# Last image's z loaded row by row of the kernel window, 32 channels outermost; its output parts in the tiles of y

## The chip, the cores and the metric

The kernel runs on one core of one Trainium2 chip. The metric is the device time of one execution in microseconds (us); the time of a kernel is the median of several runs. One profiled execution gives the trace; its span, from the first instruction to the last, is a little shorter than the time of that execution.

## What is computed

Two layers work on 16 images of 56 x 56 pixels with 384 channels. The first normalises the image in 32 groups of channels, makes q, k and v with a 1x1 convolution, lets every pixel attend to 9 neighbours (at distance 1, 2 or 3, a third of the channels each), projects the result and adds it to the image. The second normalises again, convolves each channel by itself with a 3x3 kernel of values -1, 0, 1, and adds.

```
x = x + _L0_conv_ref(_gn(x), L0_conv_w_qkv, L0_conv_w_proj, L0_conv_b_proj)
x = x + _L1_conv_ref(_gn(x), L1_conv_w)      # depthwise 3x3, 'SAME', binary kernel
```

## The kernel before

An image is cut into 7 chunks of 8 rows (PX = 448 pixels); 16 images give 112 chunks. Channels lie on the 128 partitions in 3 groups (j = 0, 1, 2). Each chunk passes three plans: plan A loads x, turns it to channels first, takes statistics and writes it to a buffer in device memory (xd); plan B is the attention and writes its result to x1d; plan C is the second layer and writes the output. Plan C of an image can only normalise when the statistics of the whole image after plan B are known.

The pieces of all plans are put on a grid of slices, sorted by slice and kind, and recorded in that order; a scheduler then orders them within each engine, and each engine works through its own list in order. So plans A and B of later images lie beside plan C of earlier ones. Only the last image (b = B - 1) has its plan C alone: nothing is left to run beside it. It fills the last 140 us of the span, and this stretch is called the tail here.

What plan C does with one chunk, with the lines:

- L745 (`load_g`) loads xg_last, the third group of channels, with a row above and below. L719 (`load_x`) loads x, the first two groups, 128 partitions of 2 x 448 values.
- `load(j)` for j = 0, 1 loads z: for each of 4 sets q of 32 channels, the same 32 channels three times, on partitions 0-31, 32-63 and 64-95, each a row of the image further (ky = 0, 1, 2). So a matmul over 96 partitions sums the three kernel rows. In the last image z has two tiles for each j, with two sets each (`z_last`); the tiles are those of t in even chunks and of w (one of xr) in odd ones, free by then. The first and the last chunk of the image are loaded by L694, one DMA for each ky and tile: 32 channels x 2 sets x 448. The chunks between are loaded by L702, one DMA for each set q, whose source pattern is written by hand with the three rows ky outermost: 3 x 32 x 448.
- L713 on ACT normalises three of the four sets of each j, L709 on DVE the fourth (q = 3); L715 on POOL clears edges in the first and the last chunk. L756 on ACT normalises xg_last into zg.
- L727 (`convolve`) is 12 matmuls for each j (24 records in the trace) into the PSUM tile pc, the q = 3 one first; L734 on DVE adds pc to x.
- L769 on DVE is the nine taps of the third group, each adding to the one before (m, at last xg_last).
- L799 (`turn`) transposes four parts of 112 pixels into pt_o, L801 on ACT copies each into osb, and in the last image L804 issues the output DMA from ACT's queue. osb is a tile of pool o_p, which has 2 buffers. pc and pt_o share three PSUM buffers.

The scheduler gives the completion of each DMA one of eight semaphores in turn, over the queues of SP and ACT together. A DMA waits until the one that had its semaphore before has landed. The built program's list shows these waits.

In the tail, PE's list is: convolve chunk c (j = 0, 1), turn chunk c - 1 (four parts), convolve chunk c + 1, and so on; at the end come the turns of chunks 5 and 6.

Of the kernel before, what the change touches and what calls it, by code (L numbers as in the profile page):

```python
# [8 lines left out]
F32 = mybir.dt.float32  # L9
# [8 lines left out]
P = 128  # L18
# [4 lines left out]
NQ = 4  # L23
ROWS = 8
SUB = 112
# [10 lines left out]
def dilated_attention_then_binary_conv(  # L36
# [28 lines left out]
    nc = tc.nc  # L65
    B, H, W, C = x.shape
    PX = ROWS * W
    NCH = H // ROWS
# [82 lines left out]
    y_p = ctx.enter_context(tc.tile_pool(name="y_p", bufs=4))  # L151
# [5 lines left out]
    o_p = ctx.enter_context(tc.tile_pool(name="o_p", bufs=2))  # L157
# [497 lines left out]
    def plan_c(m, t0):  # L655

        b, c = divmod(m, NCH)
        p0 = c * PX
        had = {}

        def edges(j):
            found = []
            for z, _, _ in had[f"z{j}"]:
                if c == 0:
                    found.append(z[0:HD, :, 0:W])
                if c == NCH - 1:
                    found.append(z[2 * HD : 3 * HD, :, PX - W : PX])
            return found

        def set_of(j, q):  # L670
            return next(z[:, q - q0] for z, q0, q1 in had[f"z{j}"] if q0 <= q < q1)

        def load(j):
            by_set = x1d[b].rearrange("(j q c) n -> j c q n", q=NQ, c=HD)[j]
            if b < B - 1:
                z = z_p.tile([P, NQ * PX], F32, tag="z", name="z")[:K3].rearrange("p (q n) -> p q n", q=NQ)
                had[f"z{j}"] = [(z, 0, NQ)]
            else:

                had[f"z{j}"] = []  # L680
                for q0 in range(0, NQ, 2):
                    pool, tag = (t_p, "t") if c % 2 == 0 else (w_p, "w") if (j, q0) != (1, 2) else (xr_p, "xr")
                    z = pool.tile([P, 3, PX], F32, tag=tag, name="z_last")[:K3, :2]
                    had[f"z{j}"].append((z, q0, q0 + 2))
            for edge in edges(j):
                nc.gpsimd.memset(edge, 0.0)
            for ky in range(3):
                lo = W if c == 0 and ky == 0 else 0
                hi = PX - W if c == NCH - 1 and ky == 2 else PX
                n0 = p0 + (ky - 1) * W  # L690
                for z, q0, q1 in had[f"z{j}"]:
                    if b == B - 1 and 0 < c < NCH - 1:
                        continue
                    nc.sync.dma_start(  # L694
                        z[ky * HD : (ky + 1) * HD, :, lo:hi], by_set[:, q0:q1, n0 + lo : n0 + hi]
                    )
            if b == B - 1 and 0 < c < NCH - 1:

                for q in range(NQ):
                    one = by_set[:, q, p0 - W : p0 - W + PX]  # L700
                    three_rows = bass.AP(one.tensor, one.offset, [(W, 3), *one.ap])
                    nc.sync.dma_start(set_of(j, q), three_rows)  # L702

        def normalise(j):
            mrz = mr1[b][1]
# [88 lines left out]
        def turn(s):  # L794
            pt = ps_mt.tile([P, 512], F32, tag="mt", name="pt_o")
            mid = had["xg"][:, 1 : ROWS + 1, :].rearrange("p r w -> p (r w)")
            for j in range(NG):
                src = mid if j == JG else had["x1"][:, j]
                nc.tensor.transpose(pt[:SUB, j * P : (j + 1) * P], src[:, s * SUB : (s + 1) * SUB], ident)  # L799
            osb = o_p.tile([SUB, C], F32, tag="osb", name="osb")  # L800
            nc.scalar.copy(osb, pt[:SUB, :C])  # L801

            queue = nc.sync if b < B - 1 else nc.scalar
            queue.dma_start(of[b, p0 + s * SUB : p0 + (s + 1) * SUB, :], osb)  # L804

        if b == B - 1:

            at(t0 - 12, LOADS, load_g)
            at(t0 - 3, LOADS, load_x)
            ahead = 8 if c else 1  # L810
            at(t0 - ahead, NORM, normalise_g)
            for j in range(JG):
                at(t0 - 12 + j, LOADS, lambda j=j: load(j))
                at(t0 - ahead + j, NORM, lambda j=j: normalise(j))
                at(t0 + 1 + j, CONVOLVE, lambda j=j: convolve(j))
            for ky in range(3):
                at(t0 + 1 + ky, CONVOLVE, lambda ky=ky: taps_last(ky))
            for s in range(NSUB):
                at(t0 + 12, STAGE_C, lambda s=s: turn(s))
            return  # L820
# [9 lines left out]
        for j in range(JG):  # L830
            at(t0 - 4 + 3 * j, LOADS, lambda j=j: load(j))
            at(t0 - 1 + 3 * j + late, NORM, lambda j=j: normalise(j))
            at(t0 + 2 + 3 * j + late, CONVOLVE, lambda j=j: convolve(j))
        for s in range(NSUB):
            at(t0 + 9 + s, STAGE_C, lambda s=s: turn(s))
# [51 lines left out]
```

## Time and profile before

| | us |
|---|---|
| median of 3 runs (lowest, highest) | 5411.35 (5409.35, 5414.15) |
| the profiled execution, its own time | 5406.89 |
| its span | 5405.2 |
| PE busy in the span | 5205.9 (96%) |
| DVE, POOL, ACT busy | 4150.0, 4215.2, 2397.8 |
| mean granted TensorE clock | 0.98 of full speed |
| normalising of the last image starts | at 5269.5 |
| convolve of chunk 1 ends (PE) | at 5293.7 |
| convolve of chunk 2, 3, 4, 5 starts | at 5300.55, 5323.03, 5345.41, 5369.80 |
| convolve of chunk 6 ends | at 5391.8 |
| last output copy starts (ACT) | at 5401.41 |

How to read the views used below. "SPq" and "ACTq" are the queues in which SP and ACT issue DMAs; the time of such a row is that of issuing, not of the transfer. In the chain of waits, each piece is what the next one waited for, followed back from the last instruction; the trace gives a landing as the time between issue and what it released. In a timeline, a row gives the start, the time until the last of its instructions ended, engine, line, operation, out<-in, and the count. PEclk is the granted share of the TensorE clock, "DMA share" the mean busy share of the 16 DMA engines.

### The profile page before, as it was taken

Reading aid. Unit: us, or ns where it says so; the run is one execution under the profiler, and the core shown is the slowest. Engines: PE = TensorE matmul, PEld = TensorE weight load, DVE = VectorE, ACT = ScalarE, POOL = GpSimd, SP = SyncE. Lnnn points to the kernel's source line nnn. Section 1 sums busy time; section 2 is a strip of 40 time slices with the busy share of each in tenths; the row PEclk is TensorE's granted clock in tenths of the full one; section 3 lists DMA queues with packets and bytes.
Section 4 is the critical chain, followed back from the end, with each engine's and each line's share of the span. In section 5 each row is a group of like instructions: output and inputs, shape, how many; then the busy total and the mean of one; then the engine's idle time right before and its main releaser. Section 6 shows DMA issues by size and latency. Waiting matters only on the chain. (4 is left out here: it accounts for less than half of the span.)

```text
span 5405.2 us, 77297 instructions
## 1 busy us (share of the span) xinstructions
PE 5205.9 (96%) x27669; PEld 2414.4 (45%) x27669; DVE 4150.0 (77%) x4209; ACT 2397.8 (44%) x4189; POOL 4215.2 (78%) x3049
## 2 busy tenths in 40 slices
PE   8999999999999999999999999999999999999965
PEld 4444444444444444444444444444444444444422
DVE  4887777878777787777777777787777778777754
ACT  3224444444444444444444444444444444444433
POOL 2677888888888887888888788888888888888880
PEclk9999999999999999999999999999999999999976
DMA  5444555655555555555655655555555655544443
GB/s 168 127 120 124 159 157 158 163 154 161 158 158 160 164 159 159 157 157 158 163 154 161 164 152 160 164 157 163 159 157 154 164 154 161 161 130 134 122 130 126
DMA packets 810799, 825.73 MB, mean 153 GB/s; under 512 B 359467, under 2 KB 800174, under 8 KB 810414
## 3 DMA queue, kind: packets, MB, share of 16 engines
q1 hardware_dynamic: 802430, 808.79, 54.2%
q10 hardware_dynamic: 7984, 12.00, 0.7%
q8 instruction: 219, 3.59, 0.3%
q14 instruction: 166, 1.36, 0.1%
HBM read 466.41 MB, written 231.21 MB: 129 GB/s over the span
## 5 line engine op out<-in xcount | busy, mean ns | idle before, releaser
L597 POOL TENSOR_TENSOR w<-w 128x1344 f32<-128x1344 f32 x672 | 2049.9, 3050 | 456.2 <-DVE w L589 396.7
L589 DVE TENSOR_TENSOR w<-pb_a,v 128x1344 f32<-128x1344 f32 x1008 | 1559.1, 1547 | 267.0 <-PE pb_a L582 177.4
L516 DVE TENSOR_TENSOR t<-pq,k 128x1344 f32<-128x1344 f32 x1008 | 1535.8, 1549 | 237.0 <-PE pq L463 236.1
L463 PE MATMUL pkv<-xn,wqkvT 128*128 128x448 f32 x3924 | 1569.9, 549 | 9.0 <-ACT xa L424 4.7
L463 PEld LDWEIGHTS pkv<-xn,wqkvT 128*128 128x128 f32 x3924 | 718.4, 190 | 671.8 <-issue 629.4
L615 PE MATMUL po<-y,wprojT 128*128 128x448 f32 x2016 | 834.9, 550 | 27.4 <-POOL y L601 15.0
L784 POOL TENSOR_TENSOR m<-m 128x1344 f32<-128x1344 f32 x210 | 644.7, 3070 | 274.1 <-ACT m L778 274.0
L463 PE MATMUL pq<-xn,wqkvT 128*128 128x448 f32 x1962 | 830.7, 558 | 0.0
L713 ACT ACTIVATE z<-z,mrz 96x448 f32<-96x448 f32 x840 | 578.3, 751 | 350.9 <-DMA z<-x1d 330.3
L501 PE MATMUL ps<-t,sel 128*32 128x448 f32 x6048 | 666.0, 550 | 26.0 <-DVE t L516 25.3
L778 ACT ACTIVATE m<-zg,ktap 128x448 f32<-128x448 f32 x945 | 555.5, 658 | 274.0 <-POOL m L784 266.9
L615 PEld LDWEIGHTS po<-y,wprojT 128*128 128x128 f32 x2016 | 376.4, 191 | 382.9 <-issue 341.1
L727 PE MATMUL pc<-z,kdiag 96*32 96x440 f32 (+1 forms) x5040 | 516.7, 543 | 6.4 <-POOL z L715 4.6
L463 PEld LDWEIGHTS pq<-xn,wqkvT 128*128 128x128 f32 x1962 | 344.0, 189 | 316.9 <-issue 316.9
L734 DVE TENSOR_TENSOR x<-pc,x 128x448 f32<-128x448 f32 x224 | 139.3, 622 | 353.2 <-PE pc L727 342.1
L582 PE MATMUL pb_a<-aT,spread 24*128 24x448 bf16 x3024 | 369.1, 359 | 32.2 <-DVE w L589 25.9
L601 POOL TENSOR_TENSOR y<-y,w 128x448 f32<-128x448 f32 x336 | 381.5, 1135 | 22.6
L618 DVE SCALAR_TENSOR_TENSOR xr<-po,bias,xr 128x448 f32<-128x448 f32 x336 | 227.5, 677 | 220.9 <-PE po L615 217.2
L600 POOL TENSOR_TENSOR y<-w 128x448 f32<-128x448 f32 x336 | 382.2, 1138 | 14.7
L473 ACT COPY v<-pkv 128x448 f32<-128x448 f32 x336 | 178.3, 531 | 484.1 <-PE pkv L463 475.8
L473 ACT COPY k<-pkv 128x448 f32<-128x448 f32 x336 | 178.2, 530 | 376.5 <-PE pkv L463 376.5
L501 PEld LDWEIGHTS ps<-t,sel 128*32 128x32 f32 x6048 | 170.6, 110 | 364.9 <-issue 247.8
(131 smaller groups left out, 4394.7 us busy)
## 6 DMA issues: line engine op xcount, KB each, us to landing
z<-x1d SPq DMA_DIRECT2D x570, 224.0 KB
xr<-xd SPq DMA_DIRECT2D x112, 672.0 KB
x1d<-xr SPq DMA_DIRECT2D x112, 672.0 KB
xn<-xd SPq DMA_DIRECT2D x109, 672.0 KB
xin<-in_x_dram SPq DMA_DIRECT2D x108, 672.0 KB
xd<-xa SPq DMA_DIRECT2D x315, 224.0 KB
out_dram<-osb SPq DMA_DIRECT2D x420, 168.0 KB
x<-x1d SPq DMA_DIRECT2D x112, 448.0 KB
```

The costliest lines, as they stand in the source:

```text
L463: nc.tensor.matmul(dst[:, :PX], wqkvT[:, cc, o0 : o0 + P], had["xn"][:, cc, :], start=(cc == 0), stop=(cc == NG - 1))
L501: return nc.tensor.matmul(had["ps"][32 * j : 32 * j + 32, :PX], sel[:, s0 : s0 + 32], tk, start=(issued[j] == 1), stop=(issued[j] == len(r ...
L516: nc.vector.tensor_tensor(t.rearrange("p k (r w) -> p k r w", w=W), q3, k3, ALU.mult)
L589: nc.vector.tensor_tensor(w.rearrange("p k (r w) -> p k r w", w=W), pb[:, :, :PX].rearrange("p k (r w) -> p k r w", w=W), three(kv[1][g][m ...
L597: nc.gpsimd.tensor_tensor(w0, w0, w, ALU.add)
L600: nc.gpsimd.tensor_tensor(y, w0[:, 0], w0[:, 1], ALU.add)
L601: nc.gpsimd.tensor_tensor(y, y, w0[:, 2], ALU.add)
L615: nc.tensor.matmul(po[:, :PX], wprojT[:, g, j * P : (j + 1) * P], had[f"y{g}"], start=(g == 0), stop=(g == NG - 1))
L713: nc.scalar.activation(z, z, AF.Identity, bias=mrz[:, j, q, 0:1], scale=mrz[:, j, q, 1:2])
L727: return nc.tensor.matmul(pcr[q * HD : (q + 1) * HD, :, lo:hi], kdiag[:, kx, j * NQ + q, :], rows(set_of(j, q))[:, :, lo + kx - 1 : hi + k ...
L778: nc.scalar.activation(rows(t[:, kx]), zp[:, ky : ky + ROWS, kx : kx + W], AF.Copy, scale=ktap[:, o : o + 1])
L784: nc.gpsimd.tensor_tensor(had["m"], had["m"], t, ALU.add)
```

## The change

In `load(j)`, the middle chunks of the last image lose their own way: the branch with the hand-written pattern (L702) and the `continue` that led to it are gone, so that all chunks go through L694. For chunks 1 to 5 that is 3 (ky) x 2 (tiles) = 6 DMAs of 32 x 2 x 448 for each j in place of 4 of 3 x 32 x 448, with the same bytes. In `turn`, the last image's osb is a view of a tile of pool y_p, which has 4 buffers and whose own use, in plan B, is over by then; other images keep o_p.

```diff
                 for z, q0, q1 in had[f"z{j}"]:
-                    if b == B - 1 and 0 < c < NCH - 1:
-                        continue
                     nc.sync.dma_start(
                         z[ky * HD : (ky + 1) * HD, :, lo:hi], by_set[:, q0:q1, n0 + lo : n0 + hi]
                     )
-            if b == B - 1 and 0 < c < NCH - 1:
-
-                for q in range(NQ):
-                    one = by_set[:, q, p0 - W : p0 - W + PX]
-                    three_rows = bass.AP(one.tensor, one.offset, [(W, 3), *one.ap])
-                    nc.sync.dma_start(set_of(j, q), three_rows)
...
-            osb = o_p.tile([SUB, C], F32, tag="osb", name="osb")
+            if b < B - 1:
+                osb = o_p.tile([SUB, C], F32, tag="osb", name="osb")
+            else:
+                osb = y_p.tile([P, PX], F32, tag="y", name="osb_last")[:SUB, :C]
             nc.scalar.copy(osb, pt[:SUB, :C])
```

In the built programs the lists of PE and POOL are the same but for two rows of POOL (clearing of edges) that change places, and the lists of DVE, ACT and SP are the same up to the start of the tail. In the tail the scheduler orders them anew. Before, the normalising of a chunk and the copies of the turn before it are mixed on ACT and on DVE. After, from chunk 2 on, ACT's list is: two copies, two output DMAs, two copies, two output DMAs (turn of chunk c - 2), six times L713 (chunk c), L756 (chunk c + 1). DVE's list is: L709 twice (chunk c), L734 (c, j = 0), three taps of chunk c + 1, L734 (c, j = 1), six taps of chunk c + 1, L709 twice (chunk c + 1). On SP's queue, a chunk is x (c), xg_last (c + 1), 12 loads of z (c + 1); the output DMAs on ACT's queue take their turn among the eight semaphores between the loads of z.

## The prediction

> **What bounds the kernel now.** Over the whole span PE is busy 96%, but only the tail is changed. I read the chain of waits from 5293 to 5345 first, because it tells what ends last there (start, time, what):
>
> ```profile
> by line: DMA z_last<-x1d 95.3%; SPq L702 4.0%; issue 1.6%; ACT osb L801 0.9%; PE pt_o L799 0.9%; ACT z_last L713 0.0%; ACTq L801 0.0%
> ...
> 5293.74 12.89 DMA z_last<-x1d
> ...
> 5306.64 25.25 DMA z_last<-x1d x2
> ...
> 5331.96 11.44 DMA z_last<-x1d
> ```
>
> Landings of z are 95% of it: the tail is bound by transfers, not by an engine. Next, busy time by engine in two whole chunks of that stretch (engines, then PEclk, DMA share, GB/s):
>
> ```profile
> 5300.50:5345.40 44.90, 23.35 (x120) 7.76 (x120) 15.76 (x26) 13.75 (x22) 0.00 (x0) 0.61 0.38 126
> ```
>
> In 44.90 us PE works 23.35, DVE 15.76, ACT 13.75, POOL nothing; the DMA engines are 38% busy on average. 38% is neither idle nor full, so SP's timeline tells how the loads are spread:
>
> ```profile
> 5302.34 23.14 SPq L702 DMA_DIRECT2D z_last<-x1d  x10
> ...
> 5328.77 21.09 SPq L702 DMA_DIRECT2D z_last<-x1d  x9
> ...
> 5370.44 6.35 SPq L694 DMA_DIRECT2D z_last<-x1d  x8
> ```
>
> Ten L702 loads need 23.14 us, 2.31 each, against 0.79 for an L694 load. The trace's semaphore updates say why: of the 16 steps of the L702 load issued at 5302.34, 13 come at once (5303.5) and three at 5313.1 to 5313.6. Three engines carry it: 96 rows of 1792 B over 3 are 32 rows, 2.31 / 32 = 72 ns per row. The x load issued at 5302.2 also lands last on those three engines, at 5310.4. So 40 loads x 2.31 = 92.6 us of three queues are the tail's length, and a chunk comes every 22 to 24 us. In the waits of the tail (engine, line, releaser: us, times, longest) the users of z show it, and last the rows for osb:
>
> ```profile
> DVE z_last L709 <- DMA z_last<-x1d: 47.3, 10, 8.0
> ACT z_last L713 <- DMA z_last<-x1d: 38.8, 18, 4.4
> ...
> ACT osb L801 <- DMA out_dram<-osb: 14.9, 10, 3.7
> ```
>
> **What the Trainium skill says.** "DMA: Bandwidth & Descriptors", section "Rules for kernel authors": an outermost dimension below 16 confines a DMA to at most that many engines; put a multiple of 16 outermost. Its section "Why a DMA increments its semaphore by 16 and not by 1": the sequencer adds the share of unused engines at once. The trace agrees: 13 at once, then 3. "TensorE: Matmul & The Clock Gate", "Part 1: The HAM clock gate": PE runs at half clock after idling until a window of some 3.4 us was busy. The trace agrees: PEclk is 0.61 in the two chunks, and it becomes full 6.7 us after convolve of chunk 1 starts (5285.70) and 4.7 us after that of chunk 5 (5369.80).
>
> **The change, part by part.**
>
> *Loads.* L702 goes (40 DMAs), L694 comes (60), each 32 outermost, thus over 16 engines. A row of 1792 B keeps its 72 ns, so 64 rows over 16 engines are 0.29 us of transfer. Four L694 loads of chunk 0 stand 0.47 us apart in the trace, and one landed 2.2 us after issue in quiet, another 3.6 under load. SP issues per chunk x, xg and 12 loads: 14 x 0.45 = 6.3 us. A chunk's bytes (z 1.38, xg 0.29, x 0.46, output 0.69 MB) are 2.81 MB; 16 rows per 72 ns are 398 GB/s, so 7.1 us. Neither binds if something else takes longer than 7.1 us.
>
> *What is late next: the engines.* I follow one chunk from the end of convolve (c - 1) to the start of convolve (c), by the new lists.
>
> DVE: L734 of j = 1 0.60 with its wait, six taps 4.28 (before: seven L769 in 5.00), L709 0.51, handover 0.07: 5.45.
>
> ```profile
> 5369.86 5.00 DVE L769 SCALAR_TENSOR_TENSOR m<-zg,ktap,m 128x448 f32<-128x448 f32 x7
> ```
>
> ACT: after the first transposes (0.58), two pairs of copies and their DMAs. A pair is 0.86 of copies with 0.80 of issuing behind the first, a cadence of 1.35; then three L713 (2.06 before for three): 0.58 + 2.7 + 2.06 and handovers is 5.4 to 5.5.
>
> ```profile
> 5392.40 0.86 ACT L801 COPY osb<-pt_o 112x384 f32<-112x384 f32 x2 [5.46 <-PE pt_o L799]
> 5392.91 0.80 ACTq L804 DMA_DIRECT2D out_dram<-osb  x2
> ```
>
> The two are level at 5.5 us. Meanwhile PE turns chunk c - 2 or waits.
>
> PE: convolve of both j took 8.04 for chunk 1, half clock for 6.7 of it:
>
> ```profile
> 5285.70 8.04 PE L727 MATMUL pc<-z_last,kdiag 96*32 96x448 f32 x48
> ```
>
> At half clock one j is 4.4 to 4.7, at full 2.2 to 2.4. With full clock some 5 us after the start, 48 records take 5 + 1.9 = 6.9. The period is 5.5 + 6.9 = 12.4 us.
>
> Does z arrive? Its loads for chunk c + 1 need the tiles of the other parity, free when convolve (c - 1) has read them. Six loads of j = 0 are issued first; the last of j = 1 waits for semaphores last used by the outputs, and lands about 8.4 us after the period's start, against 9.9 when it is used: 1.5 us of slack.
>
> *Start of the tail.* Normalising starts at 5269.5 in both. Before, DVE waited until 5282.6 for chunk 1's z; now all of it should land before 5267: SP starts on it at 5257.8, and 12 loads at some 0.5 to 0.6 us are 6 to 7 us and 2.2 to landing. DVE's list then runs without a gap: convolve of chunk 1 starts near 5280.1 and ends 5285.4 (before 5293.7). DVE's 27 taps (0.67 to 0.71), five L709 and four L734 from 5269.5 are 23 us, so chunk 2 starts at 5292.6 (before 5300.55) and ends at 5299.6. Chunks 3, 4, 5 end 12.4 apart: 5312.0, 5324.4, 5336.8. Chunk 6 takes 12.4 + 0.4 for the edges cleared by POOL: 5349.6 (before 5391.8).
>
> *osb.* Four tiles in place of two. In the middle chunks the copies waited for landings (part of the 14.9 us above), but z was later; alone this gives nothing there. After the last convolve it counts: eight copies ran from 5392.40 to 5401.89, with 0.45 to 1.83 of waiting between. With four tiles, four pairs are 5.5 us: L734 and the first turn 0.4, pairs 5.5, landing 2.1 (5401.92 to 5404.0), program end 1.2: 9.2 after the last convolve, before 13.3. The gain is 4.1. If a landing still holds the fifth copy, 1 to 2 us of it are lost.
>
> *Sum.* 5349.6 + 9.2 = 5358.8 for the span, against 5405.2: 46.4 less (some 42 by loads, 4 by osb). The profiled execution took 5406.9, 1.7 over its span: after 5360.5. The median of the runs stands 4.5 above it, so 5365.
>
> *The unknown costs, both ends.* PE's clock: a gap of 5.5 us between convolves may keep it at full, which makes convolve 4.6 and gains 2.3 x 5 = 11 us: 5354. If it stays half throughout, convolve is 9.0, +2.1 x 5 = +10: 5375. I take half at first, as every chunk of before shows it. A load under traffic: 2.2 to 3.6 us to landing; 3.6 eats the slack of 1.5 in part. The added wait: an output's turn among the eight semaphores stands between the loads of z on SP's queue, and behind that wait stand the rest of z and the next x. Before shows that such waits exist, with no data between the two:
>
> ```profile
> SPq L719 <- DMA out_dram<-osb: 3.7, 2, 3.2
> ```
>
> From both sides: 0 (the slack covers it) to 4 us per chunk. It can't gain, since it only delays. I take 0.
>
> **The rivals.**
>
> *The semaphores bind.* Outputs under load landed 4.1 us after issue (5369.29 to 5373.4). If the loads wait for both pairs of outputs in turn, each 2.0 later than a quiet landing (4.1 - 2.1), and land 1.4 later themselves (3.6 - 2.2), that is 5.4 late; less 1.5 of slack some 4 per chunk: +4 x 5 = +20 us, 5385. It decides from 1.5 us of lateness on. For: only eight semaphores are shared by 18 DMAs per chunk. Against: with 16 engines the traffic is 2.81 MB in 12.4 us, 227 of 398 GB/s, so landings should be shorter than those before, which stood behind the three engines' queues.
>
> *Nothing comes of it.* Another bound sits right behind, at 22 us per chunk: 5405 to 5411. Against: per chunk PE has 11.7, DVE 7.9, ACT 6.9 us of work, and even with no overlap but that of PE with the others (11.7 + 7.9 = 19.6) two or three us per chunk are saved.
>
> *Slower.* One mechanism: each L694 load holds the queues as long as an L702 load did, because what costs is the DMA and not its rows. 60 x 2.31 = 138.6 against 92.6: +46, 5457. It decides from 92.6 / 60 = 1.54 us per load on. For: no row of before has L694 loads at the rate that the change asks for. Against: in chunk 6's row above a load takes 0.79, and in this one, ahead of the tail, 0.58:
>
> ```profile
> 5224.72 1.73 SPq L694 DMA_DIRECT2D z_last<-x1d  x3
> ```
>
> Both lie well below 1.54.
>
> **How the numbers follow.** Forecast 5365, its own range 5354 to 5375 by the clock: chance 0.78. Semaphores bind, 5385: 0.15. Nothing, 5405 to 5411: 0.03. Slower, 5457: 0.04. The range is 5352 (full clock and a landing saved at the end) to 5386, with 0.07 and the forecast's own edges left out. A measurement of this kernel can tell about 0.2%, 10.8 us, from no change. Faster is 0.78 + 0.15 = 0.93, same 0.03, slower 0.04.
>
> **What would show it.** Right: SP issues 12 L694 rows per middle chunk, under 0.8 us each; the semaphore steps of one show 16 landings; convolves of chunks 2 to 6 start about 12.4 apart; the chain of waits in the middle of the tail names DVE L769, L709, ACT L713, L801 and PE L727 in turn and hardly a z landing; PEclk there lies near 0.7; no wait for out_dram<-osb on ACT before the last chunk; the end is 9 us after the last convolve. Wrong: if the chain still names z landings with SP waiting for out_dram<-osb, the semaphores bind; if DVE and ACT wait for z with loads over 1.5 us apart, the loads cost as before. A convolve of 4.6 us means the clock stayed full, of 9 that it stayed half. The prediction fails if engines are slowed by each other's traffic, which the quiet tail of before does not show.

## The result, and the profile after

| | before | after |
|---|---|---|
| median of 4 runs (lowest, highest), us | 5411.3 (5409.35, 5414.15) | 5372.8 (5370.18, 5376.01) |
| ratio, 95% interval | | 0.9929 [0.9912, 0.9946] |
| profiled execution, us; its span | 5406.89; 5405.2 | 5376.01; 5374.3 |
| normalising of the last image starts (DVE), at | 5269.53 | 5277.12 |
| from there to the end of the span ("tail") | 135.6 | 97.2 |
| end of convolve 1 to end of convolve 6 (five chunks) | 98.2 | 69.5 |
| end of convolve 6 to end of the span | 13.3 | 8.8 |

The medians differ by 38.5 us, the tails by 38.4. The forecast was 46.4 less, 5365; the range held. The profiled execution of after reaches the tail 7.6 us later than that of before, though the engines' lists are the same up to there; an offset like this differs between executions (the start lies between 5269.5 and 5280.8 in the runs below), so all stages below are counted from the start of the normalising.

The change removes eight lines, so L702/L694 of before is L692 after; L709 is L701, L713 L705, L727 L719, L734 L726, L745 L737, L756 L748, L769 L761, L799 L791, L801 L796, L804 L799.

The timeline of SP for one chunk (start, us, queue, line, count), first, and then two rows of the waits of SP between 5300 and 5365 (us, times, longest):

```profile
5330.44 0.34 SPq L737 DMA_DIRECT2D xg_last<-x1d  x1
5330.88 11.67 SPq L692 DMA_DIRECT2D z_last<-x1d  x12
5343.44 0.38 SPq L711 DMA_DIRECT2D x<-x1d  x1
```

```profile
SPq L692 <- DMA out_dram<-osb_last: 14.4, 6, 4.1
SPq L692 <- DMA xg_last<-x1d: 8.4, 4, 3.6
```

Twelve loads take 11.67 us, but not because each is dear: in the trace one follows another after 0.4 to 0.5 us where nothing is waited for. The rest is mostly the waits of the second fence: the loads stand behind landings of outputs and of xg_last, from which they take no data; only the semaphore is the same. The semaphore of a load (the one issued at 5331.36) now takes 16 single steps, from 5334.8 to 5336.7: all 16 engines carry it. The landings of z themselves, as the waits of the tail have them, fell from 38.8 us (ACT) and 47.3 us (DVE) to this:

```profile
ACT z_last L705 <- DMA z_last<-x1d: 5.8, 4, 2.8
DVE z_last L701 <- DMA z_last<-x1d: 5.7, 4, 2.5
```

PE's timeline shows what a chunk costs now. In brackets stands the idle time ahead of the row and what ended it:

```profile
5302.60 8.01 PE L719 MATMUL pc<-z_last,kdiag 96*32 96x448 f32 x48 [4.86 <-DVE z_last L701]
...
5317.22 7.53 PE L719 MATMUL pc<-z_last,kdiag 96*32 96x448 f32 x48 [3.79 <-ACT z_last L705]
...
5330.14 7.89 PE L719 MATMUL pc<-z_last,kdiag 96*32 96x448 f32 x48 [3.79 <-ACT z_last L705]
```

A convolve takes 7.5 to 8 us; between the end of one and the start of the next lie 6.6, 6.6, 5.4, 6.6 and 5.7 us, of which the turn fills some 2. The busy times of three whole chunks:

```profile
5302.60:5344.60 42.00, 28.36 (x181) 15.69 (x182) 24.46 (x39) 20.11 (x33) 1.10 (x5) 0.74 0.74 206
```

PEclk is 0.74, and the DMA engines are busy 0.74 at 206 GB/s. So full use at this mix of transfers would be 206 / 0.74 = 278 GB/s, and a chunk's 2.81 MB cost 10.1 us of all engines: much nearer to the period of 13.9 than the forecast had it.

The chain of waits from 5300 to 5352 names PE's convolve first and the landings of z with 3.1% (95.3% before); landings of xg_last and of the outputs have taken a part of their place:

```profile
by line: PE pc L719 39.1%; DMA xg_last<-x1d 12.3%; DMA out_dram<-osb_last 9.4%; issue 8.1%; DVE m L761 8.0%; ACT z_last L705 7.0%; ACT osb_last L796 5.8%; DMA z_last<-x1d 3.1%; PE pt_o L791 2.9%; ACTq L799 2.4%; ACT zg L748 1.7%; DVE x L726
```

One stretch of it has the longer gap (some pieces left out):

```profile
5298.84 2.60 DMA out_dram<-osb_last
...
5301.48 0.43 SPq L692
...
5302.49 6.38 DMA xg_last<-x1d
...
5308.96 0.86 ACT zg L748
...
5309.85 0.70 DVE m L761
...
5311.97 0.54 DVE x L726
...
5312.56 0.55 PE pt_o L791 x3
...
5315.28 1.41 ACT z_last L705 x2
...
5317.22 7.53 PE pc L719 x48
```

An output lands, the load that has its semaphore is issued, xg_last only behind it; it lands 6.4 us later and zg follows. Three taps stand ahead of L726 in DVE's list, the second half of the turn waits for L726, ACT's copies wait for the turn, and the normalising waits for the copies.

### The profile page after: what moved, and what is told of

It is laid out like the page before. It is cut to its first block, busy times and chain, and to the rows that moved or that the text cites. A ratio compares the mean times of both kernels' runs of the same rounds, so it can differ in the third digit from the quotient of the medians.

```text
span 5374.3 us, 77362 instructions
## 1 busy us (share of the span) xinstructions
PE 5199.5 (97%) x27669; PEld 2420.8 (45%) x27669; DVE 4151.0 (77%) x4209; ACT 2397.5 (45%) x4189; POOL 4216.7 (78%) x3049
## 5 line engine op out<-in xcount | busy, mean ns | idle before, releaser
L705 ACT ACTIVATE z<-z,mrz 96x448 f32<-96x448 f32 x840 | 578.2, 751 | 355.5 <-DMA z<-x1d 337.2
L719 PE MATMUL pc<-z,kdiag 96*32 96x440 f32 (+1 forms) x5040 | 520.0, 546 | 6.4 <-POOL z L707 4.4
L726 DVE TENSOR_TENSOR x<-pc,x 128x448 f32<-128x448 f32 x224 | 139.4, 622 | 354.8 <-PE pc L719 352.2
```

The source lines that it names most:

```text
L705: nc.scalar.activation(z, z, AF.Identity, bias=mrz[:, j, q, 0:1], scale=mrz[:, j, q, 1:2])
L719: return nc.tensor.matmul(pcr[q * HD : (q + 1) * HD, :, lo:hi], kdiag[:, kx, j * NQ + q, :], rows(set_of(j, q))[:, :, lo + kx - 1 : hi + k ...
```

## The experiments

All are built on the changed kernel, except e2 and e3, which start from before. "Five chunks" is from the end of convolve 1 to that of convolve 6, "end" what follows.

| kernel | median, us | ratio to before, 95% | tail | five chunks | end |
|---|---|---|---|---|---|
| e1_loads_alone | 5373.65 | 0.9928 [0.9913, 0.9942] | 99.3 | 70.1 | 13.0 |
| e2_osb_alone | 5404.23 | 0.9986 [0.9979, 0.9993] | 131.5 | 96.0 | 11.3 |
| e3_two_and_one | 5413.2 | 1.0000 [0.9992, 1.0009] | 137.5 | 107.5 | 9.0 |
| e4_act_first | 5375.56 | 0.9935 [0.9920, 0.9950] | 101.5 | 73.5 | 9.0 |
| e5_both_first | 5368.34 | 0.9920 [0.9903, 0.9936] | 96.2 | 68.1 | 8.8 |
| e6_busy_pe | 5394.29 | 0.9964 [0.9951, 0.9977] | 119.4 | 91.5 | 8.8 |
| e7_out_pool | 5372.54 | 0.9929 [0.9915, 0.9944] | 96.7 | 66.2 | 11.4 |
| e8_busy_pe_short | 5366.33 | 0.9917 [0.9902, 0.9931] | 89.4 | 64.3 | 8.8 |
| e9_first_and_pool | 5368.48 | 0.9913 [0.9896, 0.9930] | 94.3 | 67.9 | 9.8 |
| e10_first_and_x | 5371.04 | 0.9918 [0.9901, 0.9935] | 96.1 | 67.8 | 8.9 |
| e11_first_x_pool | 5366.68 | 0.9912 [0.9896, 0.9928] | 96.3 | 67.2 | 9.8 |
| e12_dve_order | 5361.08 | 0.9901 [0.9885, 0.9918] | 86.0 | 57.2 | 11.3 |

The tail has a scatter of its own: convolve 0 takes 7.0 to 7.1 us in before, e1, e2, e3, e8 and e9 and 9.7 to 9.9 in the others, with and without edits near it. "Five chunks" is free of that, but each is one profiled execution: the convolves 2 to 6 of e7, whose edit does not touch them, take 1.6 us less in sum than those of after, so differences of one or two us are not told apart. Differences in the text are taken before rounding. (The expectations count the tail of after as 97.8.)

**The two parts alone.** e1 takes back this part of the change; e2 is the kernel before with this part alone.

```diff
-            if b < B - 1:
-                osb = o_p.tile([SUB, C], F32, tag="osb", name="osb")
-            else:
-                osb = y_p.tile([P, PX], F32, tag="y", name="osb_last")[:SUB, :C]
+            osb = o_p.tile([SUB, C], F32, tag="osb", name="osb")
```

> The changed loads alone; the output parts stay in the two tiles of o_p. From the start of normalising the last image to the end of the span the kernel before needs 135.7 us, the changed one 97.8. Theory (four tiles count only after the last convolve, 4.1 us): 102 us, and a time of some 5377, 0.9936 of before. Rival (with loads fast, the copies' wait for a free tile becomes a bound in every chunk): 1 to 3 us more in each of five chunks, 107 to 117 us, 5382 to 5392.

> The output parts in the tiles of y alone; the loads of three rows (3 outermost) stay. Theory (loads bind until the last convolve, the tiles count after it): 4 us less than before, 131.7 us of tail, some 5407. Rival (the waits of the copies for a landing are on the path in the middle chunks too): 8 us or more less.

e1: the end is 13.0 in place of 8.8, and five chunks take 70.1 against 69.5: the tiles act after the last convolve, by 4.2 us, and hardly before. The tail is only 2.1 longer than after's, because convolve 0 happens to be 2.7 shorter; the two medians can't tell such a difference. e2: 4.1 less in the tail, the theory's size, but not all in its place: the end is 2.0 shorter (11.3), and 1.9 come in chunk 6, from the end of convolve 5 to that of convolve 6 (13.2 in place of 15.1), whose loads went through L694 before too. The loads alone take 36.3 us off the tail (135.6 to 99.3).

**Is it the outermost dimension?**

```diff
-                    three_rows = bass.AP(one.tensor, one.offset, [(W, 3), *one.ap])
-                    nc.sync.dma_start(set_of(j, q), three_rows)
+                    two_rows = bass.AP(one.tensor, one.offset, [(W, 2), *one.ap])
+                    nc.sync.dma_start(set_of(j, q)[: 2 * HD], two_rows)
+                    nc.sync.dma_start(set_of(j, q)[2 * HD :], by_set[:, q, p0 + W : p0 + W + PX])
```

> As e2_osb_alone, but each load of 3 x 32 rows is cut in two: one of 2 x 32 rows (2 outermost) and one of 32 rows (32 outermost). Theory (the outermost dimension sets the number of engines, each row takes 72 ns there): the load of 64 rows is held by two engines, again 32 rows each, 2.31 us; 40 of them are again 92.6 us: the same tail as e2_osb_alone within 3 us, though a third of the bytes now goes over 16 engines. Rival 1 (what is slow is slow by its bytes): two thirds of 92.6, 31 us less. Rival 2 (each DMA costs the queue its 2.3 us whatever its shape): 40 more DMAs, some 90 us more.

Both rivals fall. A third of the bytes moved to loads with 32 outermost, and the tail became 6.0 longer than e2's, not 31 shorter; the forecast of 3 was short of that. The semaphore steps say where the 6 come from. The two-row load issued at 5321.56 makes its last two steps at 5329.4 and 5329.9. The 32-row load issued next, at 5322.10, has 14 parts landed by 5324.0 and the last two at 5329.6 and 5330.1: a wide load puts two of its rows on each of the two engines that the narrow loads have filled. As an estimate, 40 x 2 x 72 ns = 5.8 us. (Five chunks alone grow by 11.5, because convolve 1 ends 3.1 earlier than in e2 and the end is 2.3 shorter.)

**Is PE's clock the next thing?** After each turn of chunks 0 to 4, matmuls that nobody reads:

```diff
+            if b == B - 1 and s == NSUB - 1 and c < NCH - 2:
+                idle = ps_s.tile([P, 512], F32, tag="s", name="idle")
+                flat = kdiag.rearrange("p a b c -> p (a b c)")[:, :PX]
+                for i in range(16):
+                    tc.keep_in_program_order(
+                        nc.tensor.matmul(idle[:HD, :PX], kdiag[:, 1, 0, :], flat, start=(i == 0), stop=(i == 15))
+                    )
```

> The changed kernel with 16 further matmuls of the convolve's size after each turn of chunks 0 to 4 of the last image; nobody reads their result. They fill PE's gap of 3.8 us ahead of the next convolve. Theory (the convolves of 7.5 to 8.0 us are mostly at half clock because of that gap, and the gap is set by DVE and ACT): the clock stays full, a convolve falls to 4.6 to 5, 10 to 15 us less than the changed kernel, 83 to 88 us of tail. Rival 1 (loads, held by the semaphores of the outputs, are what chunk after chunk waits for): the convolve is shorter but the gap longer by as much, less than 4 us gained. Rival 2 (the clock stays half in spite of it, and the matmuls stand in the way): 0 to 10 us more.

e6 missed by its own price: 16 matmuls are 32 records of 0.37 us, 11.7 us, thrice the gap, since they stand one behind another where a convolve has four side by side. PE is busy throughout and PEclk is 1.00, so the convolves show what full clock is worth: 48 records in 6.1 us, the last 43 in 4.97. e8 is the same with 5 matmuls.

> As e6_busy_pe with 5 further matmuls in place of 16: each showed 0.73 us there at full clock, so 3.7 us, what PE's gap has after the turn. There the convolve at full clock took some 5 us. Theory (clock): convolves of 5 in place of 7.5 to 8.0 us and gaps as before, 10 to 14 us less than the changed kernel, 83 to 87 us of tail. Rival (a shorter convolve leaves the loads too little time): the gaps grow by the same 2.5 us, less than 4 us gained.

The clock went up (0.96), and three of the convolves take 4.9 to 5.0 us, but gaps grew to 6.6 to 7.8: five chunks gain 5.1 of the 10 to 14. The chain shows a loop that closes once in every chunk:

```profile
5312.28 4.62 DMA xg_last<-x1d
...
5316.99 0.86 ACT zg L748
...
5317.88 0.69 DVE m L761
...
5320.00 0.54 DVE x L726
...
5320.59 0.55 PE pt_o L791 x3
...
5321.68 2.79 DMA out_dram<-osb_last
...
5324.97 0.02 SPq L737
...
5325.02 4.97 DMA xg_last<-x1d
```

From one xg_last to the next are 12.7 us: landing, zg, three taps, L726, turn, copy, output's landing, and by the shared semaphore the issue of the next x and xg_last. There is no PE work of weight in it, so no clock can shorten it. This is the prediction's first rival, just behind the engines.

**Are the engines' lists the gap?** In e4, ACT's copies of a turn are queued behind the normalising of the chunk two later (`tc.issue_after`); in e5, six taps on DVE behind the next chunk's L701 as well.

```diff
+            first = on_act.get((c + 2, 0)) if b == B - 1 else None
+            with tc.issue_after(first.ins) if first else ExitStack():
+                nc.scalar.copy(osb, pt[:SUB, :C])
...
+            first = on_dve.get((c + 1, 0)) if ky else None
+            with tc.issue_after(first.ins) if first else ExitStack():
```

> The changed kernel, with ACT's order in the tail changed: all normalising of a chunk (L713 of before) stands ahead of the output copies of the turn two chunks earlier, so that it runs while PE convolves. DVE keeps its order. The changed kernel's gaps between convolves are 6.6, 6.6, 5.4, 6.6 and 5.7 us. Theory (DVE's six taps and L709 hold the convolve for 5.45 us after the one before, level with ACT): the gaps fall to about 5.5 only, 2 to 4 us less than the changed kernel, 93 to 95 us of tail. Rival (ACT alone makes the gap, DVE has slack): gaps of 3 us or less, 12 us or more less.

e4's edit did less on ACT and more on DVE than its expectation says: on ACT only one half's normalising came ahead of the copies, and the scheduler put all nine taps behind L726 (here L729; L764 are the taps, L702 the normalising). From the second on, the gaps are 7.4 to 7.6, and DVE's timeline shows them:

```profile
5321.90 0.62 DVE L729 TENSOR_TENSOR x<-pc,x 128x448 f32<-128x448 f32 x1 [1.67 <-PE pc L722]
5322.44 0.68 DVE L764 SCALAR_TENSOR_TENSOR m<-zg,ktap,xg_last 128x448 f32<-128x448 f32 x1
5323.15 5.01 DVE L764 SCALAR_TENSOR_TENSOR m<-zg,ktap,m 128x448 f32<-128x448 f32 x7
5328.19 0.69 DVE L764 SCALAR_TENSOR_TENSOR xg_last<-zg,ktap,m 128x448 f32<-128x448 f32 x1
5328.80 0.93 DVE L702 TENSOR_SCALAR z_last<-z_last,mrz 96x448 f32<-96x448 f32 x2
```

The convolve starts at 5329.40, while ACT had normalised by 5327.2. Three taps more than in the changed kernel are 2.1 us: DVE's list does set the gap.

> As e4_act_first, and on DVE the normalising of the next chunk's first half (j = 0, q = 3) stands ahead of the last six taps as well. Theory (gap bound by engines, loads with slack): the convolve starts 2 to 3 us after the one before, the period falls from 13.6 to 9 to 10.5 us (DVE has 7.9 of work, ACT 6.9 and 1.6 of issuing), 15 to 20 us less than the changed kernel, 77 to 83 us of tail. Rival (z's loads, each waiting for a semaphore of an output, bind just behind the engines): the waits for z take the gap's place, 6 us less or nothing.

My theory fell: 1.4 us. With DVE out of the way the landings bind at once, as the rival said (chain of waits, 5300 to 5350):

```profile
by line: DMA out_dram<-osb_last 33.7%; DMA z_last<-x1d 16.6%; ACT z_last L706 10.4%; DMA xg_last<-x1d 10.4%; DVE m L766 9.5%; SPq L693 6.5%; ACT osb_last L803 6.4%; issue 4.0%; ACTq L806 1.8%; ACT zg L751 1.6%; DVE x L729 1.1%; ACTq L706 0.
```

The order of ACT also has a cost of its own: the copies now stand behind a normalising that waits for z, and the last part of PE's turn waits for the copies, idle for 4.1 to 4.5 us ahead of convolves 2, 3 and 4. All runs built on e5 keep that order.

**What holds the loads?** e7 issues the outputs from POOL, which takes them off the shared semaphores.

```diff
-            queue = nc.sync if b < B - 1 else nc.scalar
+            queue = nc.sync if b < B - 1 else nc.gpsimd
```

> The changed kernel with the last image's output DMAs issued by POOL in place of ACT: they leave the eight semaphores that they share with the loads, and ACT's queue. Theory (the semaphores only delay xg_last, which makes the gaps of 6.6 where others are 5.4): two or three gaps shrink by 1.1, 2 to 4 us less than the changed kernel before what POOL's issuing costs at the end, 94 to 96 us of tail. Rival (the loads that wait for a landing output are what a chunk waits for): gaps of 4 us or less, 8 us or more less.

The gaps are 5.4 to 5.8 from the second on, and five chunks are 3.2 us shorter. That is the theory's size, but only half of it comes from the gaps (1.6 in sum); the other half are shorter convolves. POOL issues one in 0.52 us and a later start makes the end 2.6 longer, so the time stays. In this trace x is issued at 5313.96, just after the turn (two tiles of x), with xg_last and twelve loads of z behind it on the queue. So there may be two waits in one place, the semaphore and the tile. e9 is e5 with the outputs of chunks 0 to 4 on POOL; e10 is e5 with x and xg_last of chunks 3 and 5 in a tile of z_p; e11 has both.

```diff
+                if c in (3, 5):
+                    had["both"] = z_p.tile([P, NQ * PX], F32, tag="z", name="x_xg_last")
+                    xg = had["both"][:, JG * PX :]
...
+            if "both" in had:
+                x1 = had["both"][:, : JG * PX].rearrange("p (j n) -> p j n", j=JG)
```

> e5_both_first, and the outputs of the last image's chunks 0 to 4 are issued by POOL. New theory after the last four runs: beside the engines' gap there is a second bound at the same height, on SP's queue: x of a chunk waits for the turn two chunks earlier (two tiles) and for the semaphore of that turn's outputs, and xg_last and all of the next z stand behind it; with that wait the DMA engines, 75% busy in the changed kernel, can't fill the rest. Here one of its two waits (semaphores) and the engines' gap are gone, the wait for the turn stays: 2 to 6 us less than e5_both_first (96.2 us of tail), 90 to 94. Rival (the semaphores alone are the second bound): periods near 10 us, 12 to 18 us less.

> e5_both_first, and x and xg_last of chunks 3 and 5 lie in a tile of z_p of their own, so that no load of chunks 3 to 6 waits for the turn just done; the outputs stay on ACT's queue with the shared semaphores. Theory (two waits in one place, each held by the other): 0 to 6 us less than e5_both_first, 90 to 96 us of tail. Rival (the two tiles of x alone are the second bound): 10 us or more less.

> e5_both_first with both: outputs of chunks 0 to 4 on POOL, and x and xg_last of chunks 3 and 5 in tiles of their own. Theory: SP's loads run without a stop, the chunk costs what the transfers need: 75% of 13.3 us in the changed kernel is 10 us; four or five chunks at 10 to 10.5 in place of 13.3 are 12 to 16 us less than the changed kernel, 81 to 86 us of tail. Rival (transfers slow each other, or a third bound lies at 12 to 13 us): less than 5 us gained.

e9 and e10 gain nothing over e5 in five chunks (67.9 and 67.8 against 68.1): for e10 that is the edge of what was expected, for e9 it is less. In each, SP waits for what the other frees. From 5295 to 5350 these are SP's longest waits in e9:

```profile
SPq L714 <- PE pt_o L796: 12.9, 4, 3.8
```

and in e10:

```profile
SPq L748 <- DMA out_dram<-osb_last: 13.2, 4, 4.1
```

In e11 the wait for the turn is 2.4 us in that stretch. But e9 has e11's trouble with DVE too (gaps of 3.2 to 3.7 us, holes of 1.7 to 2.1 us in three convolves), so how much the tiles of x alone are worth isn't shown: e9 with the order of e12 was not run.

e11 missed; its rival's size came true (2.3 us less than after in five chunks), by a third bound. Its loads do run almost without a stop: the DMA engines are busy nine tenths or more in nearly every slice until 5338, at 295 GB/s from 5300 to 5336, and have nothing left from 5339 on. But my own order for DVE was the bound: two gaps of 3.3 us, and two convolves of 9.0 and 9.5 with a hole of 2.06 us in them, where the second half's L702 stands behind six taps. The gap of 7.2 ahead of the last chunk is DVE's too: POOL cleared the edge at 5349.07, after waiting 9.34 us for an L702 that stood behind eight taps. Chunk 4's outputs, which the next expectation blames, POOL issued only after that, at 5349.62.

> e11_first_x_pool with DVE's order changed further: both normalisings of the next chunk stand ahead of all nine taps of the chunk before it, so that a convolve waits for no tap; chunk 4's outputs go back to ACT's queue, since POOL's edge for the last chunk waited behind them (gap of 7.2 us). In e11 the loads ran ahead of their use (DMA engines busy 9 tenths or more until 5334 us, then idle), and gaps were 3.3 us, but a convolve took 9 to 9.5 us, 2 of it waiting for the second half's normalising behind six taps. Theory (with loads set free, DVE's order was what was left): gaps of about 2 us (the turn alone), convolves of 5 to 7, a period of 8 to 10 us set by DVE's 7.9 us of work or the transfers; the taps of the last chunk now end 4 to 6 us later. In sum 82 to 88 us of tail, 10 to 15 us less than the changed kernel. Rival (transfers, at most 295 GB/s in e11, hold the chunk at 12 us once the lead is used up): 92 us or more.

e12 queues both halves' normalising ahead of all nine taps:

```diff
-            first = on_dve.get((c + 1, 0)) if ky else None
+            first = None if c == 0 else on_dve[c + 1, 1] if c < NCH - 1 else on_tap[c - 1]
...
+                nxt = on_tap[c - 1] if not j else on_dve[c + 1, 1] if c < NCH - 1 else on_tap[c]
+            with tc.issue_after(nxt.ins) if nxt else ExitStack():
+                nc.vector.tensor_tensor(x1[:, j], pc[:, :PX], x1[:, j], ALU.add)
```

57.2 us for five chunks, 12.3 less than after; the median is 11.7 below after's, the lowest of all. The tail of 86.0 is as expected, but not the way to it: the gaps are 5.9, 6.1, 6.0, 3.0 and 4.4 us and not 2. Ahead of convolves 2, 3 and 4 the turn waits 3.8, 3.8 and 2.1 us for ACT's copies, and these stand behind a normalising of z that has only just landed. The window of the loaded stretch, then two shorter ones in it:

```profile
5295.00:5335.00 40.00, 30.99 (x227) 14.32 (x231) 30.02 (x49) 23.27 (x41) 9.51 (x20) 0.79 0.98 274
...
5300.00:5302.00 2.00, 2.00 (x16) 0.52 (x12) 1.89 (x4) 0.00 (x0) 0.00 (x0) 0.61 1.02 400
5303.00:5308.00 5.00, 1.46 (x14) 0.60 (x6) 1.36 (x3) 3.05 (x5) 0.00 (x0) 1.00 1.05 229
```

In this stretch the transfers are the bound: 0.98 busy at 274 GB/s, 10.3 us for a chunk's 2.81 MB. Five chunks at 11.4 each are near that. Full use is not one rate, though. From 5300 to 5302, with xg_last and outputs among what moves, it is 400 GB/s. From 5303 to 5308, where almost nothing but loads of z is under way (xg_last has landed by 5303.1, the next x lands from 5309.1), it is 229 GB/s, with the engines just as busy: as an estimate, 16 x 1792 B / 229 GB/s = 125 ns for a row. A load of z writes 32 partitions, one of x or xg_last 128; whether that is the cause no run tests. Loading fewer bytes (each row of the image is read three times) was not tried either.

## Why the prediction was right, and what it missed

The forecast's span from the start of the normalising was 5358.8 - 5269.5 = 89.3 us; it measured 97.2. Its steps:

- *The old loads are the tail's length, by three engines.* Right: the tail does not get shorter in e3, with a third of the bytes gone from them. "DMA: Bandwidth & Descriptors", section "Rules for kernel authors", is borne out: an outermost 2 is held to two engines and as slow as an outermost 3. One detail of the reading is off: 5302.2 is the first step of the x load's semaphore; the load was issued at 5298.68, and its last three steps come from 5310.05 to 5310.39.
- *New loads 0.45 apart.* Right; landing took 3.1 us in the median (2.2 to 3.6 foreseen), but 5.8 for xg_last.
- *A gap of 5.5 us, DVE and ACT level.* Right in kind. The gaps ahead of convolves 2 to 6 sum to 30.9, the forecast to 29.6 (7.2, three of 5.5, 5.9): 1.3 more. The step that failed in it is "I take 0" for the wait on the semaphores: xg_last came late by it, and two gaps were 1.1 longer.
- *Convolve 6.9 us, full clock after 5.* Too short: 8.0, 7.5, 7.9, 7.5, 7.7, together 4.1 more. The granted clock became full 5.5 to 6.6 us after the start (5302.60 to 5309.2, 5344.60 to 5350.1). I took a value near the low one out of before and not the middle: 4.7, and 6.9 by the clock's own record (5285.70 to 5292.57), where the prediction read 6.7. "TensorE: Matmul & The Clock Gate", "Part 1: The HAM clock gate", says that its window of 3.4 us is free-running; the changes in the traces do lie multiples of 3.4 apart. But the page puts the warm-up at some 3.4 us; these starts took longer, and the measurement decides. Chunk 6 of e5 had full clock only after 8.3 us (5352.47 to 5360.73), and chunk 6 of e9 and of e11 ran all of its 9.5 us at half. So the phase of the window is not all of it; what else decides is open.
- *Chunk 1's convolve ends 15.9 us after the start.* It was 18.9. Some 2.6 of it is convolve 0 at 9.7 us in place of 7.1, by the scatter named above: in e1, with convolve 0 at 7.0, convolve 1 ends after 16.1. In after, the second half of convolve 0 ran at half clock. Why the clock came late there is not shown.
- *osb gives 4.1 at the end and nothing before.* Right beside the new loads, where e1 shows 4.2 at the end. With the old ones (e2) the sum is the same, but only 2.0 of it lies at the end. The end took 8.8 (9.2 foreseen).

Sum: 4.1 + 1.3 + 3.0 - 0.4 = 8.0, against 7.9 missed. The largest is the clock term, mis-sized. All but the last err the same way, so the range did not hold by errors that cancel. That the engines stayed the bound is in part luck: the forecast had 7.1 us of transfers under a period of 12.4, the runs have 10.1 us of transfers (after) and a loop over the semaphores of 12.7 us (e8) under 13.9.

Of the rivals, "nothing" and "slower" are out; an L694 load holds the queue for 0.45 us. "The semaphores bind" was half true: not +4 us in each chunk, but a loop of 12.7 us (e8), right behind the engines' 13.9, so that lifting one thing alone was worth little in five chunks (the engines' order in e5 1.4 us, the semaphores in e7 3.2, the clock in e8 5.1); e12, with the loads free and DVE's order mended, gains 12.3. The step "7.1 us for a chunk's transfers" was wrong by 3: the chunk's mix takes 10.1 us (after) to 10.3 us (e12). It is not that 16 engines can't move the 398 GB/s, which e12 shows for 2 us; the loads of z by themselves are slower. At 13.9 it didn't bind; in e12 it does.

## What to carry to other kernels

Put a multiple of 16 outermost in a hand-written source pattern (here 32 in place of 3), and look at the semaphore's steps in the trace: a load that ends on two or three engines delays every wide load that shares them. When a bound goes and the gain stops short, list all loops that close at about the new period, before repairing one: here the engines' order, the shared semaphores (with the two tiles of x), and the transfers lay between 10 and 14 us, and the large gain came only in e12, where the first two were lifted together. Price the clock after a gap with the whole range that the traces show, here from 2.1 us at half clock (e12, convolve 3) to a whole convolve (e9 and e11, chunk 6). And measure the rate of transfers for the shape that will be moved, not for another shape.

## What the runs showed of the hardware that I had not expected

- All 16 engines at full use moved 274 GB/s in e12 and 295 GB/s in e11 (5300 to 5336) over a mix of transfers: 400 GB/s with xg_last and outputs among them, 229 GB/s in loads of z that each write 32 partitions (e12).
- The TensorE clock stayed at half through a whole convolve of 9.5 us without a pause in it (e9 and e11, chunk 6).
- A matmul of 96 x 32 by 448 in f32 takes 0.73 us alone at full clock (e6: 32 records of 0.37); in a convolve four of them side by side make 48 records in about 4.9 us, 0.10 each (e8).
- Outputs issued by POOL landed 5.4 us after issue in the median (e7) against 2.3 from ACT's queue (after); in e7 all four of a chunk come at once, together with the loads, so how much of it is POOL's way of issuing is open.
